# The masked softmax of a graph attention layer: subtraction and exponential by pairs of heads or by single heads

## The chip, the cores and the metric

The kernel runs on one NeuronCore of one Trainium2 chip. The metric is the device time of one execution in microseconds (us). One execution was taken by the hardware profiler; times in the trace count from the start of its span.

The engines are called as the profile calls them: PE is TensorE (PEld its weight loads), DVE is VectorE, ACT is ScalarE, POOL is GpSimd, SP is the engine whose queue issues the DMAs. A `q` behind the name is the engine's sequencer, which waits and issues.

## The reference

64 graphs of 256 nodes with 512 features each pass four layers. Every layer normalises the rows, applies relu, and adds its result to the rows. The change lies in the second layer, an attention with 8 heads over the graph's edges:

```python
feats = jnp.einsum('bnf,hfu->bhnu', X, W)
e_self = jnp.einsum('bhnu,hu->bhn', feats, a_self)
e_neigh = jnp.einsum('bhnu,hu->bhn', feats, a_neigh)
dense = e_self[..., :, None] + e_neigh[..., None, :]
dense = jax.nn.leaky_relu(dense, negative_slope=0.2)
dense = dense + NEG_BIG * (1.0 - A[:, None, :, :])
att = jax.nn.softmax(dense, axis=-1)
out = jnp.einsum('bhij,bhju->bhiu', att, feats) + b[None, :, None, :]
...
return jax.nn.relu(out)
```

All data are float32. The softmax runs over j, the neighbours of node i.

## The kernel before

The program is fully unrolled over the 64 graphs. The work of a graph is cut into 209 named steps; each step is a Python function that emits one or a few instructions. A table (`TIMES`) gives every step a due time; the steps of graph b are due `b * PERIOD` later, so several graphs are under way at once, one in each layer. `Plan.run` emits all steps in the order of their due times, with tables of their own for the first nine and the last eight graphs, and ties each engine's instructions to that order. [...]

Tiles come from pools (`g.take`) and go back (`g.done`) when their last user has run. Waits between engines follow from which slices of a tile an instruction writes and reads.

In the attention the eight heads are handled as four pairs, p = 0 to 3, with heads h = 2p + s for s = 0, 1. For a pair the tile `e{p}` holds 2 heads x 2 halves of the 256 neighbours j (128 partitions each) x 256 nodes i: 128 partitions x 1024 columns. The steps on it, with their lines:

- `ea{p}` (L1445, ACT): four instructions, leaky relu of the sum of the two scores, one for each head and half.
- `eg{p}` (L1453, POOL): two instructions of 512 columns, one for each head, add the mask (`negt`).
- `eb{p}` (L1459, DVE): one instruction of 1024 columns subtracts the maxima, which lie in the tile `m{p // 2}` (one row of 256 for each head, read twice, for both halves).
- `ex{p}` (L1465, ACT): one instruction of 1024 columns, the exponential.
- `po{p}` (L1477, PE): four matmul calls, which the profile shows as eight instructions, multiply with the features; in the order half 0 head 0, half 0 head 1, half 1 head 0, half 1 head 1.
- `eh{p}` (L1488, POOL): one instruction adds the two halves of both heads, for the softmax's sums; `su{q}` (L1502, PE) goes on with them.

The maxima are found without forming the scores: `max0` to `max3` (L1407, DVE) take them over masked neighbour scores, and they travel by DRAM to all partitions (`mr`, `mb0`, `mb1`).

The order of the pairs in the steady table is not the order of p. Around the change each engine's own order is, for the graphs between the first nine and the last eight (steps of other layers belong to other graphs):

- DVE: `tv0` (L1658, products of the third layer, read from PSUM), `eb2`, `sq1` (L1012, transposes of the normalised rows), `eb0`, `eb1`, `eb3`, `xe1` (L1560), `xe2` (L1565), `xe3` (L1570), `sqo`/`sqy` transposes (L1270), later `sq0` (L1012) and, some 15 us further on, `fe4` (L1368).
- ACT: `hn1` (L1103, the normalised rows of the second layer), `ex2`, `ta0` (L1665, tanh of the third layer), `ex0`, `ex1`, `ex3`, then `sm0`, `sx0` and `rs0` (L1072, L1082, L1088), the normalisation of a later graph's rows, and `hn0`.
- POOL: `pw1`, `sh1` (L1092, L1097, L1098: scale and shift of the normalisation, on two columns), `eg1` (L1453), `eh0`, `eh1` (L1488), `gsa` (L1172, L1173), `pw0`, `sh0`.
- PE: a product of the third layer, `po2`, `py0` (L1648), `po0`, `po1`, `po3`, `su0`, then products of the other layers (L1188).

Of the kernel before, what the change touches and what calls it, by code (L numbers as in the profile page):

```python
# [10 lines left out]
AF = mybir.ActivationFunctionType  # L11
OP = mybir.AluOpType
# [4 lines left out]
P = 128  # L17
D = 512
KC = D // P
N = 256  # L20
NC = N // P
# [705 lines left out]
class Graph:  # L727
# [5 lines left out]
    def step(self, name):  # L733
        def add(run):
            self.steps[name] = run
            return run
        return add
# [21 lines left out]
def tile_four_gnn_layers(ctx: ExitStack, tc: tile.TileContext, x, adj, nodemask,  # L759
# [6 lines left out]
    nc = tc.nc  # L766
# [253 lines left out]
    def graph(b):  # L1020

        g = Graph(plan)
# [415 lines left out]
        def attention(p):  # L1438
            @step(f"ea{p}")
            def _():  # L1440
                e = g.take("pair", 2, name=f"e{p}")
                for s in range(2):
                    h = 2 * p + s
                    for j in range(NC):
                        nc.scalar.activation(e[:, s, j, :], g[f"s{h // HA}"][:, h % HA, :], AF.Prelu,  # L1445
                                             bias=st["ec"][:, j, H + h:H + h + 1], alpha=0.2)
                g.done(f"s{p // 2}")

            @step(f"eg{p}")
            def _():  # L1450
                e = g[f"e{p}"]
                for s in range(2):
                    nc.gpsimd.tensor_tensor(e[:, s], e[:, s], g["negt"], OP.add)  # L1453
                g.done("negt")

            @step(f"eb{p}")
            def _():
                e = g[f"e{p}"]
                nc.vector.tensor_tensor(e, e, g[f"m{p // 2}"][:, p % 2 * 2:p % 2 * 2 + 2, None, :].to_broadcast([P, 2, NC, N]),  # L1459
                                        OP.subtract)  # L1460
                g.done(f"m{p // 2}")

            @step(f"ex{p}")
            def _():
                nc.scalar.activation(g[f"e{p}"], g[f"e{p}"], AF.Exp)  # L1465


            @step(f"po{p}")
            def _():
                e, q = g[f"e{p}"], p // 2  # L1470
                if p % 2 == 0:
                    g.take("bank", name=f"o{q}")
                po = g[f"o{q}"].rearrange("p (r n) -> p r n", r=2)
                for j in range(NC):
                    for s in range(2):
                        h = 2 * p + s
                        nc.tensor.matmul(po[s * U:(s + 1) * U, p % 2, :],  # L1477
                                         g[f"feats{j}"][:, E + h * U:E + (h + 1) * U],
                                         e[:, s, j, :], start=(j == 0), stop=(j == NC - 1))
                g.done(f"e{p}")  # L1480
                for j in range(NC):
                    g.done(f"feats{j}")


            @step(f"eh{p}")
            def _():
                e = g[f"e{p}"]
                nc.gpsimd.tensor_tensor(g.take("half", name=f"h{p}"), e[:, :, 0, :], e[:, :, 1, :], OP.add)  # L1488
                g.done(f"e{p}")
# [273 lines left out]
```

## Time and profile before

| | |
|---|---|
| time before | 3662.05 us, median of 3 runs (3653.04 to 3664.11) |
| profiled execution | 3662.73 us, its span 3660.9 us |
| granted TensorE clock, mean over the span | 0.981 |
| instructions in the trace | 61887 |
| idle time ahead of L1477 (PE) until L1465 has ended | 99.4 us, 58 times |
| idle time ahead of L1465 (ACT) until L1459 has ended | 28.7 us, 25 times |
| idle time ahead of L1488 (POOL) until L1465 has ended | 128.8 us |
| DMA | 785.31 MB, mean 215 GB/s |

How to read the profile's lines. A line of a group names the source line, the engine, the operation, the tiles out<-in, the shape and the count; then follow the busy time in us and the mean duration of one instruction in ns; then the idle time of the engine just before these instructions and what ended most of it. A line of the waits says who waited for whom: us in total, how many times, and the longest wait. A line of the timeline has the start in us, the length in us of all the instructions merged in the line, the engine, line and operation, the count, and in square brackets the idle time before it with what ended it. A busy engine in these lists can also be one whose instruction has started and is held up.

### The profile page before, as it was taken

To read this page: it belongs to the slowest core of one execution; us is meant where nothing else is said; L and a number is where in the kernel's file an instruction comes from. 1 tells how busy PE (TensorE), PEld (TensorE's weight loads), DVE (VectorE), ACT (ScalarE), POOL (GpSimd) and SP (SyncE) were. 2 spreads that over 40 slices of the span, in tenths; PEclk is the share of its full clock that TensorE was granted. 3 is DMA by queue.
4 is the path that set the end of the run, shared out by engine and by line. 5 is a ranking of instruction groups with operands and counts; after the bars stand their busy time and mean duration, and the time that the engine had idled before them with its cause. 6 is when DMAs were issued, how large, how long until landed. Compare 5 with 4: busy or idle time off the path is not lost.

```text
span 3660.9 us, 61887 instructions
## 1 busy us (share of the span) xinstructions
PE 3404.0 (93%) x16834; PEld 2175.1 (59%) x16834; DVE 3278.9 (90%) x8248; ACT 2780.4 (76%) x6533; POOL 2313.9 (63%) x2708
## 2 busy tenths in 40 slices
PE   5688999999999999999999999999999999999988
PEld 3455655666666666666666666666666666555554
DVE  6789998999999999999999999999989999999985
ACT  2667787787787788788778778778778778777765
POOL 3565666666666666676676666666666666566663
PEclk8789999999999999999999999999999999999999
DMA  6667667777777777777777777777777777777663
GB/s 187 181 183 216 203 215 219 222 222 222 224 219 221 228 226 218 231 222 226 219 224 221 230 223 222 228 222 221 224 219 225 223 223 229 208 212 216 197 191 119
DMA packets 995146, 785.31 MB, mean 215 GB/s; under 512 B 791984, under 2 KB 862192, under 8 KB 994800
## 3 DMA queue, kind: packets, MB, share of 16 engines
q1 hardware_dynamic: 994800, 781.35, 70.9%
q8 instruction: 137, 2.24, 0.2%
q14 instruction: 209, 1.71, 0.1%
HBM read 511.12 MB, written 270.01 MB: 213 GB/s over the span
## 4 chain that ended last, share of the span: by engine, by line
DVE 20%; PE 19%; POOL 18%; issue 13%; DMA 11%; ACT 7%; SPq 5%; POOLq 0%; ACTq 0%; DVEq 0%
PE bank L1188 13%; DMA big<-sq_d 6%; SPq L1017 4%; DVE junk L1407 4%; DVE big L1459 3%; POOL big L1453 3%; DVE big L1202 3%; PE bank L1477 3%; DVE big L1012 2%; POOL rstd L1092 2%; POOL big L1173 2%; POOL big L1172 2%; DMA sq_d<-big 2%; POOL big L1179 2%; POOL mid L1488 2%
## 5 line engine op out<-in xcount | busy, mean ns | idle before, releaser
L1188 PE MATMUL bank<-t_s,big 128*128 128x264 f32 (+3 forms) x3072 | 978.9, 452 | 8.0 <-DVE big L1658 5.7
L1188 PE MATMUL bank<-w_s,big 128*128 128x264 f32 (+2 forms) x3072 | 847.1, 409 | 44.5 <-DMA big<-sq_d 35.7
L1188 PEld LDWEIGHTS bank<-t_s,big 128*128 128x128 f32 x3072 | 582.0, 193 | 308.2 <-issue 176.7
L1188 PEld LDWEIGHTS bank<-w_s,big 128*128 128x128 f32 x3072 | 582.1, 195 | 273.9 <-issue 131.0
L1453 POOL TENSOR_TENSOR big<-big,mid 128x512 f32<-128x512 f32 x512 | 649.0, 1294 | 42.9 <-ACT big L1445 33.0
L1012 DVE STREAM_TRANSPOSE big<-big 128x512 f32<-128x512 f32 x640 | 483.5, 782 | 147.1 <-ACT big L1103 147.0
L1092 POOL TENSOR_TENSOR rstd<-rstd,power 128x2 f32<-128x2 f32 x256 | 183.6, 717 | 641.0 <-ACT rstd L1088 584.3
L1103 ACT ACTIVATE big<-big,shift,rstd 128x512 f32<-128x512 f32 x512 | 387.8, 805 | 171.7 <-POOL shift L1098 171.2
L1172 POOL TENSOR_TENSOR big<-big 128x256 f32<-128x256 f32 x256 | 226.6, 885 | 437.3 <-DMA big<-sq_d 288.1
L1407 DVE CUSTOM_DVE_ANT_0 junk<-big,bank 128x256 f32<-128x256 f32 x1024 | 428.9, 419 | 33.9 <-DMA big<-er_d 2.8
L1488 POOL TENSOR_TENSOR mid<-big 128x512 f32<-128x512 f32 x256 | 376.1, 1490 | 128.9 <-ACT big L1465 128.8
L1082 ACT ACTIVATE big<-big,sum 128x512 f32<-128x512 f32 x512 | 363.8, 711 | 111.4 <-DVE sum L1333 82.6
L1445 ACT ACTIVATE big<-big,ec 128x256 f32<-128x256 f32 x1024 | 428.8, 496 | 3.8 <-DMA big<-er_d 1.2
L1202 DVE TENSOR_TENSOR big<-bank,big 128x320 f32<-128x320 f32 (+1 forms) x704 | 399.2, 571 | 23.2 <-PE bank L1188 17.9
L1477 PE MATMUL bank<-big,big 128*64 128x256 f32 x2048 | 261.6, 390 | 103.8 <-ACT big L1465 99.4
L1459 DVE TENSOR_TENSOR big<-big,big 128x1024 f32<-128x1024 f32 x256 | 326.0, 1312 | 6.5 <-DMA big<-m_d 6.3
L1634 PE MATMUL bank<-big,big 64*128 64x256 f32 x2048 | 286.0, 400 | 45.9 <-DVE mx L1407 27.4
L1658 DVE TENSOR_TENSOR big<-bank,mid 128x512 f32<-128x512 f32 x512 | 320.9, 679 | 0.8 <-PE bank L1634 0.7
L1665 ACT ACTIVATE big<-big 128x512 f32<-128x512 f32 x512 | 291.3, 619 | 13.3 <-DVE big L1658 10.9
L1634 PEld LDWEIGHTS bank<-big,big 64*128 64x128 f32 x2048 | 221.6, 198 | 127.4 <-ACT big L1622 58.7
L1465 ACT ACTIVATE big<-big 128x1024 f32<-128x1024 f32 x256 | 267.9, 1052 | 38.0 <-DVE big L1459 28.7
L1537 ACT ACTIVATE big<-big,rs 128x64 f32<-128x64 f32 x1024 | 257.4, 334 | 27.1 <-DVE rs L1526 13.7
(132 smaller groups left out, 5839.8 us busy)
## 6 DMA issues: line engine op xcount, KB each, us to landing
sq_d<-big SPq DMA_DIRECT2D x448, 512.0 KB
big<-sq_d SPq DMA_DIRECT2D x1792, 128.0 KB
big<-er_d SPq DMA_DIRECT2D x256, 512.0 KB
big<-m_d SPq DMA_DIRECT2D x128, 512.0 KB
big<-in_x_dram SPq DMA_DIRECT2D x64, 512.0 KB
out_dram<-big SPq DMA_DIRECT2D x64, 512.0 KB
mid<-in_adj_dram SPq DMA_DIRECT2D x64, 256.0 KB
mid<-in_adj_dram SPq DMA_DIRECT2D x256, 64.0 KB
```

The costliest lines, as they stand in the source:

```text
L1012: nc.vector.transpose(sq.rearrange("p (r k i c) -> p c k r i", r=4, k=KC, c=NC)[:, c], t[:, c])
L1082: nc.scalar.activation(g["hn"][:, c, :], g["xt"][:, c, :], AF.Square, scale=-float(D), bias=st["sum"][:, c:c + 1], accum_out=st["ssq"][:, ...
L1103: nc.scalar.activation(g["hn"][:, c, :], g["xt"][:, c, :], AF.Relu, bias=st["shift"][:, c:c + 1], scale=st["rstd"][:, c:c + 1])
L1188: nc.tensor.matmul(p, a()[:, k], w[:, k], start=(k == 0), stop=(k == 1))
L1202: nc.vector.tensor_tensor(out(), g[i][:, :w], old(), OP.add)
L1407: nc.vector.tensor_tensor_reduce(junk, g[f"n{h // HA}"][:, h % HA, :], g["far"][:, c * N:(c + 1) * N], 1.0, -BIG, OP.add, OP.max, g["mx"][ ...
L1445: nc.scalar.activation(e[:, s, j, :], g[f"s{h // HA}"][:, h % HA, :], AF.Prelu, bias=st["ec"][:, j, H + h:H + h + 1], alpha=0.2)
L1453: nc.gpsimd.tensor_tensor(e[:, s], e[:, s], g["negt"], OP.add)
L1459: nc.vector.tensor_tensor(e, e, g[f"m{p // 2}"][:, p % 2 * 2:p % 2 * 2 + 2, None, :].to_broadcast([P, 2, NC, N]), OP.subtract)
L1477: nc.tensor.matmul(po[s * U:(s + 1) * U, p % 2, :], g[f"feats{j}"][:, E + h * U:E + (h + 1) * U], e[:, s, j, :], start=(j == 0), stop=(j = ...
L1488: nc.gpsimd.tensor_tensor(g.take("half", name=f"h{p}"), e[:, :, 0, :], e[:, :, 1, :], OP.add)
L1634: nc.tensor.matmul(ps[s][:, m, :], chunk(g["xpt"][half, p], m), g["xc"][half, p, :], start=True, stop=True)
```

## The change

`eb{p}` and `ex{p}` loop over the two heads of the pair. Each subtraction and each exponential now covers one head, 512 columns, and there are two of each where there was one. The order of the steps, the tiles, the values and all else stay.

```diff
             @step(f"eb{p}")
             def _():
                 e = g[f"e{p}"]
-                nc.vector.tensor_tensor(e, e, g[f"m{p // 2}"][:, p % 2 * 2:p % 2 * 2 + 2, None, :].to_broadcast([P, 2, NC, N]),
-                                        OP.subtract)
+                for s in range(2):
+                    m = g[f"m{p // 2}"][:, p % 2 * 2 + s, None, :]
+                    nc.vector.tensor_tensor(e[:, s], e[:, s], m.to_broadcast([P, NC, N]), OP.subtract)
                 g.done(f"m{p // 2}")
 
             @step(f"ex{p}")
             def _():
-                nc.scalar.activation(g[f"e{p}"], g[f"e{p}"], AF.Exp)
+                for s in range(2):
+                    nc.scalar.activation(g[f"e{p}"][:, s], g[f"e{p}"][:, s], AF.Exp)
```

## The prediction

> **What bounds the kernel now.** I read the page first: which engines are full, and what stands before and behind the two changed lines.
>
> ```profile
> PE 3404.0 (93%) x16834; PEld 2175.1 (59%) x16834; DVE 3278.9 (90%) x8248; ACT 2780.4 (76%) x6533; POOL 2313.9 (63%) x2708
> ...
> L1459 DVE TENSOR_TENSOR big<-big,big 128x1024 f32<-128x1024 f32 x256 | 326.0, 1312 | 6.5 <-DMA big<-m_d 6.3
> ...
> L1658 DVE TENSOR_TENSOR big<-bank,mid 128x512 f32<-128x512 f32 x512 | 320.9, 679 | 0.8 <-PE bank L1634 0.7
> L1665 ACT ACTIVATE big<-big 128x512 f32<-128x512 f32 x512 | 291.3, 619 | 13.3 <-DVE big L1658 10.9
> ...
> L1465 ACT ACTIVATE big<-big 128x1024 f32<-128x1024 f32 x256 | 267.9, 1052 | 38.0 <-DVE big L1459 28.7
> ```
>
> TensorE and VectorE are both nearly full, so neither alone is the answer. The instruction list of L1459 shows that the first of a graph's four subtractions starts at 706.00 us in graph 11 and at 3043.80 in graph 54, 54.37 us apart on average, and that the four keep their distances within about 0.02 us in these 44 graphs. One period can therefore stand for them; I take the one from 1467.38 to 1521.55. Its waits:
>
> ```profile
> ACT big L1103 <- POOL shift L1098: 2.7, 2, 1.4
> DVE big L1012 <- ACT big L1103: 2.6, 2, 1.4
> ...
> PE bank L1477 <- ACT big L1465: 1.4, 1, 1.4
> ...
> DVE bank L1368 <- PE bank L1188: 0.4, 1, 0.4
> ```
>
> TensorE's longest wait is for an exponential; VectorE waits for the normalised rows, which wait for GpSimd; and at L1368 VectorE waits 0.4 us for TensorE. After that VectorE runs with no wait of note to the next period. So whatever makes TensorE later at the attention makes L1368 later and the period longer, one for one. Now the timeline of the attention, engine by engine (start, length of the whole line, count):
>
> ```profile
> 1467.47 1.18 POOL L1097 TENSOR_TENSOR shift<-sum,rstd 128x2 f32<-128x2 f32 x1
> 1468.73 0.20 POOL L1098 TENSOR_TENSOR shift<-shift,share_of 128x2 f32<-128x2 f32 x1
> ...
> 1473.64 3.49 POOL L1488 TENSOR_TENSOR mid<-big 128x512 f32<-128x512 f32 x2 [2.25 <-ACT big L1465]
> ```
> ```profile
> 1467.38 1.22 DVE L1459 TENSOR_TENSOR big<-big,big 128x1024 f32<-128x1024 f32 x1
> 1469.81 1.42 DVE L1012 STREAM_TRANSPOSE big<-big 128x512 f32<-128x512 f32 x2 [1.21 <-ACT big L1103]
> 1471.15 3.59 DVE L1459 TENSOR_TENSOR big<-big,big 128x1024 f32<-128x1024 f32 x3
> ```
> ```profile
> 1468.96 1.52 ACT L1103 ACTIVATE big<-big,shift,rstd 128x512 f32<-128x512 f32 x2 [1.31 <-POOL shift L1098]
> 1470.39 1.04 ACT L1465 ACTIVATE big<-big 128x1024 f32<-128x1024 f32 x1
> 1471.34 1.14 ACT L1665 ACTIVATE big<-big 128x512 f32<-128x512 f32 x2
> 1472.51 3.33 ACT L1465 ACTIVATE big<-big 128x1024 f32<-128x1024 f32 x3
> ```
> ```profile
> 1471.48 1.08 PE L1477 MATMUL bank<-big,big 128*64 128x256 f32 x8 [1.44 <-ACT big L1465]
> ...
> 1474.12 2.93 PE L1477 MATMUL bank<-big,big 128*64 128x256 f32 x24
> ```
>
> The point to see: L1097 is an instruction on two columns, mostly 0.20 us, but here it lasts 1.18 us and ends just after eb2, which started 0.09 us before it. The first L1488 (eh0) starts 0.11 us after eb3 (1473.53) and ends 1.15 us after it. GpSimd and a subtraction of two SBUF operands exclude each other. Who gets in when two subtractions stand back to back is shown early in the run:
>
> ```profile
> 196.29 5.64 DVE L1459 TENSOR_TENSOR big<-big,big 128x1024 f32<-128x1024 f32 x3
> ```
> ```profile
> 196.67 4.17 POOL L1453 TENSOR_TENSOR big<-big,mid 128x512 f32<-128x512 f32 x2
> ```
>
> Three subtractions take 5.64 us and not 3.59: single ones take 1.18, 2.31 and 2.30, and the two L1453 run in the two gaps. A waiting GpSimd instruction goes in at the boundary, and the next subtraction pays 1.10 us (2.31 less the median of 1.21). In all eleven places where a GpSimd instruction of 256 or 512 columns waited at such a boundary, it went first. The change puts a new boundary into every subtraction.
>
> **The change part by part.**
>
> Instructions. 256 VectorE instructions become 512 and 256 ScalarE instructions become 512; nothing else is added, removed or reordered, no DMA, and no queue is passed. A subtraction of 512 columns I take from L1658: 0.68 us, the next starting 0.60 later (four in 2.47 us). A pair lasts 1.28 against 1.21: 0.07 more. No row has the subtraction itself at 512; the ends are half of its 1.21 (a pair then costs nothing) and L1063, 512 columns with two SBUF operands, whose 805 ns contain the times it is held up (a pair then costs 0.4). L1658 is the nearest in operation and size, so I take it. An exponential of 512 is like L1665: 0.61, the next after 0.52 (two in 1.13 to 1.14). A pair lasts 1.13 against 1.04, but its first half is there 0.43 earlier. Were each 0.07 on the path, 256 would cost 18 us; on ScalarE 256 times 0.09 is 23 us, but ScalarE is 76% busy.
>
> The first head, eb2 to po2. L1097 no longer waits for all of eb2. The first half ends at 1468.06, L1097 gets in and ends 0.05 later, at 1468.11. L1098 comes 0.08 later and finds the second half (1467.98 to 1468.66) at work; it ends 0.05 after that, 1468.71, against 1468.93 now. So hn1 and all that follows start 0.21 earlier (1468.75 instead of 1468.96). Po2's first products can start after one half; the last wait for the second half, 1470.70 to 1471.32. TensorE leaves po2 0.34 us earlier (six of eight products left at 1471.37, 0.11 each, against eight at 1471.48).
>
> eb0, eb1, eb3. From 1470.94 (1471.15 less 0.21), with the 0.10 that L1453 holds up eb0 now, the halves start at 1470.94, 1471.64, 1472.24, 1472.84, 1473.44 and 1474.04; undisturbed the last ends at 1474.72, where it ends now (1474.74). ScalarE: ex2 at 1470.18 and 1470.70, L1665 at 1471.22 and 1471.74, ex0 at 1472.26 and 1472.78 to 1473.39; eh0 comes 0.08 after that, at 1473.47, some 0.02 after the first half of eb3. It waits for that half (to 1474.12) and then runs ahead of the second half. Today nothing of VectorE that reads two SBUF operands stands behind eb3, so the same wait costs VectorE nothing. Then, the second half of eb3 ends at 1474.04 + 0.68 + 1.10 = 1475.82, 1.08 later than now. Queued behind it on VectorE are xe1 to xe5 and the transposes (L1560, L1565, L1270); VectorE has 1.4 us of idle time before L1012 at 1481.01, which covers 1.08. Ex3's second half runs 1475.85 to 1476.48 instead of ending at 1475.84: ScalarE is 0.64 later, and with it sm0, sx0, rs0 and hn0, for which VectorE waits at 1481.01. Po3 now starts its eight products at 1475.88; then its last six start at 1476.53, and TensorE is free at 1477.19 against 1476.76: 0.43 later. That has eaten the 0.34 that po2 gave.
>
> The meeting point. At L1368 VectorE comes 0.64 later but had waited 0.41, so it is 0.23 late; TensorE is 0.43 late. The later one counts: 0.43 us per period. In 44 graphs that is 19 us. In the other 20 the order differs; the like waits there (eh0 held 0.55 to 0.7 us by eb3 in graphs 4 to 7) bound them by 0 and by about 1 us each, and I take the same 0.43: 9 us. Sum 28 us. The profiled execution took 3662.7 us (span 3660.9), 0.7 from the median of 3662.05, so 3662 + 28 = 3690.
>
> A rule against this reading: the Trainium skill (Perfetto Trace Analysis, Optimizing Scalar/DVE Operations) says that where ScalarE and VectorE aren't saturated but cause bubbles on other engines, breaking up instructions may let work finish sooner. By it the 1.44 us bubble before po2 should shrink and the sum be a gain, some 15 us by the 0.34 above; with VectorE at 90% its condition hardly holds, and the rows of 196.29 decide for me.
>
> **Rivals.**
>
> 1. eh0 gets in one boundary earlier. My margin is 0.02 us. For: a subtraction at 3274.91 yielded to a GpSimd instruction that started 0.05 before it. Against: at 252.89 one won against an L1098 that had started 0.02 to 0.03 before. Then both halves of eb3 pay 1.10 (eh0 ahead of the first, eh1 ahead of the second): eb3 ends 2.2 later, ex3 1.76, TensorE 1.53 late at L1368. 44 times 1.53 is 67 us, with 0.5 for each of the others 77: 3739.
>
> 2. Faster: GpSimd does not get in between the halves. The next VectorE instruction starts 0.08 before its predecessor ends, which could close the gap for shorter ones. Then eb3 ends as now, ex3 ends 0.43 earlier, po3 follows po1 0.34 earlier, and each period is 0.34 shorter: 15 us in 44 graphs, 22 in all 64, 3640 to 3647. It decides as soon as eb3 pays less than 0.43 us. Against: eleven of eleven.
>
> 3. The loss is mostly covered. If TensorE recovers its 0.43 before L1368, VectorE's own 0.23 stays: 10 to 15 us, or, with some graphs untouched, under the 11 us (0.3%) that a measurement of this kernel can tell from no change. Against: TensorE has no wait between po3 and 1489.5.
>
> 4. The exponential still waits for both halves, so that the overlap does not arise. Against: L1665 starts at 1515.33, before the second L1658 of its pair ends at 1515.84, with the same slices by head. Ex3 would end 0.5 us later still (0.52 and 0.61 after 1475.85), 22 us in 44 graphs: about 3715.
>
> **How the numbers follow.** Forecast 0.50 (with small shifts about it, 3675 to 3710), rival 1 0.18, rival 4 0.05, rival 3 0.14, rival 2 0.13. Predicted 3690. The range runs from 3655, which leaves out most of rival 2, to 3745, above rival 1 with its unknown 20 graphs. Below 3651 lies rival 2: 0.13; within 0.3%: most of rival 3: 0.12; the rest is slower: 0.75.
>
> **What would show it.** Right: L1459 x512 with a mean of 0.8 to 0.9 us and not 0.68, a second half of eb3 near 1.8 us, L1097 after eb2 near 0.65 us, hn1 starting 1.37 us after eb2 (now 1.58), a period near 54.8 us, L1488 with a shorter mean. Wrong: all halves at 0.68 (rival 2), or both halves of eb3 at 1.8 (rival 1), or a changed period while eb3 is undisturbed.

## The result and the profile after

The changed kernel takes 3690.86 us (median, 3688.71 to 3695.31); the kernel before, on the same chip in the same comparison, 3658.78. The ratio is 1.0084, 95% interval 1.0071 to 1.0097: 0.8% slower. The prediction was 3690 us. The profiled execution took 3695.31 us with a span of 3693.5, at a mean granted clock of 0.984 (before: 3662.73, 3660.9, 0.981). From 700 to 3050 us it is 1.00 in both, so the clock is no part of the loss. All lines behind the change shift by two.

The page after, engines and groups:

```profile
PE 3433.0 (93%) x16834; PEld 2137.8 (58%) x16834; DVE 3354.7 (91%) x8504; ACT 2795.9 (76%) x6789; POOL 2300.8 (62%) x2708
...
L1461 DVE TENSOR_TENSOR big<-big,big 128x512 f32<-128x512 f32 x512 | 414.2, 866 | 7.2 <-DMA big<-m_d 7.1
...
L1467 ACT ACTIVATE big<-big 128x512 f32<-128x512 f32 x512 | 289.1, 618 | 78.6 <-DVE big L1461 78.3
...
L1660 DVE TENSOR_TENSOR big<-bank,mid 128x512 f32<-128x512 f32 x512 | 320.7, 677 | 0.9 <-PE bank L1636 0.5
```

Two VectorE instructions of the same size stand here. L1660, with one operand in PSUM, keeps its 0.68 us. L1461, with both in SBUF, has a mean of 866 ns. An undisturbed L1461 takes 0.68 too (below), so the mean holds time in which it was held up. The exponential waits 78.3 us for it instead of 28.7.

The graph whose first subtraction starts at 1479.75, on VectorE, GpSimd, ScalarE and TensorE in turn (start, length of the whole line, count):

```profile
1479.75 1.28 DVE L1461 TENSOR_TENSOR big<-big,big 128x512 f32<-128x512 f32 x2
1481.97 1.42 DVE L1012 STREAM_TRANSPOSE big<-big 128x512 f32<-128x512 f32 x2 [0.94 <-ACT big L1103]
1483.31 4.88 DVE L1461 TENSOR_TENSOR big<-big,big 128x512 f32<-128x512 f32 x6
```
```profile
1479.84 0.65 POOL L1097 TENSOR_TENSOR shift<-sum,rstd 128x2 f32<-128x2 f32 x1
1480.56 0.52 POOL L1098 TENSOR_TENSOR shift<-shift,share_of 128x2 f32<-128x2 f32 x1
...
1485.84 3.49 POOL L1490 TENSOR_TENSOR mid<-big 128x512 f32<-128x512 f32 x2 [2.29 <-ACT big L1467]
```
```profile
1484.63 2.69 ACT L1467 ACTIVATE big<-big 128x512 f32<-128x512 f32 x5
1488.22 0.63 ACT L1467 ACTIVATE big<-big 128x512 f32<-128x512 f32 x1 [0.90 <-DVE big L1461]
```
```profile
1488.91 1.08 PE L1479 MATMUL bank<-big,big 128*64 128x256 f32 x6 [0.46 <-ACT big L1467]
1489.91 0.64 PE L1504 MATMUL bank<-mid,ones 128*32 128x256 f32 x8
```

The gain is there: L1097 lasts 0.65 instead of 1.18, as it goes in between the two halves of eb2. So is the loss: six halves of eb0, eb1 and eb3 need 4.88 us where three whole subtractions needed 3.59. Five exponentials run without a gap, then ScalarE waits 0.90 for the last half of eb3, and TensorE waits 0.46 for that exponential.

Over graphs 11 to 54 the instruction list of L1461 gives a period of 54.837 us; before it was 54.367. In the medians of these graphs the second half of eb3 takes 1765 ns and each other half 678 to 682, except the first of eb0, which L1453 holds up (789). The span is 32.6 us longer: 43 periods of 0.47 make 20.2, graphs 0 to 11 add 5.1, graphs 54 to 63 8.6, and the ends take off 1.2.

### The profile page after: what moved, and what is told of

Read it like the earlier page. It is cut to its first block, busy times and chain, and to the rows that moved or that the text cites. A ratio compares the mean times of both kernels' runs of the same rounds, so it can differ in the third digit from the quotient of the medians.

```text
span 3693.5 us, 62315 instructions
## 1 busy us (share of the span) xinstructions
PE 3433.0 (93%) x16834; PEld 2137.8 (58%) x16834; DVE 3354.7 (91%) x8504; ACT 2795.9 (76%) x6789; POOL 2300.8 (62%) x2708
## 4 chain that ended last, share of the span: by engine, by line
DVE 24%; PE 20%; POOL 19%; issue 14%; DMA 11%; ACT 7%; SPq 5%; POOLq 0%; DVEq 0%; ACTq 0%
PE bank L1188 15%; DVE big L1461 7%; DMA big<-sq_d 7%; SPq L1017 4%; DVE junk L1407 4%; POOL big L1453 3%; DVE big L1012 3%; POOL rstd L1092 3%; DVE big L1202 2%; POOL big L1173 2%; POOL big L1172 2%; POOL big L1179 2%; POOL big L1180 2%; ACT big L1082 2%; POOL mid L1490 2%
## 5 line engine op out<-in xcount | busy, mean ns | idle before, releaser
L1188 PE MATMUL bank<-t_s,big 128*128 128x264 f32 (+3 forms) x3072 | 978.2, 452 | 6.9 <-DVE big L1660 5.5
L1188 PE MATMUL bank<-w_s,big 128*128 128x264 f32 (+2 forms) x3072 | 849.0, 409 | 43.4 <-DMA big<-sq_d 36.1
L1188 PEld LDWEIGHTS bank<-t_s,big 128*128 128x128 f32 x3072 | 580.4, 193 | 308.4 <-issue 191.8
L1188 PEld LDWEIGHTS bank<-w_s,big 128*128 128x128 f32 x3072 | 577.8, 195 | 279.8 <-issue 154.8
L1453 POOL TENSOR_TENSOR big<-big,mid 128x512 f32<-128x512 f32 x512 | 648.4, 1292 | 46.3 <-ACT big L1445 34.4
L1490 POOL TENSOR_TENSOR mid<-big 128x512 f32<-128x512 f32 x256 | 375.0, 1485 | 138.9 <-ACT big L1467 137.0
L1461 DVE TENSOR_TENSOR big<-big,big 128x512 f32<-128x512 f32 x512 | 414.2, 866 | 7.2 <-DMA big<-m_d 7.1
L1479 PE MATMUL bank<-big,big 128*64 128x256 f32 x2048 | 316.2, 392 | 102.3 <-ACT big L1467 99.6
L1467 ACT ACTIVATE big<-big 128x512 f32<-128x512 f32 x512 | 289.1, 618 | 78.6 <-DVE big L1461 78.3
L1660 DVE TENSOR_TENSOR big<-bank,mid 128x512 f32<-128x512 f32 x512 | 320.7, 677 | 0.9 <-PE bank L1636 0.5
L1667 ACT ACTIVATE big<-big 128x512 f32<-128x512 f32 x512 | 291.3, 618 | 12.7 <-DVE big L1660 10.6
L1479 PEld LDWEIGHTS bank<-big,big 128*64 128x64 f32 x2048 | 166.1, 138 | 232.6 <-ACT big L1467 172.0
```

Source lines behind the costliest of these rows:

```text
L1188: nc.tensor.matmul(p, a()[:, k], w[:, k], start=(k == 0), stop=(k == 1))
L1461: nc.vector.tensor_tensor(e[:, s], e[:, s], m.to_broadcast([P, NC, N]), OP.subtract)
L1479: nc.tensor.matmul(po[s * U:(s + 1) * U, p % 2, :], g[f"feats{j}"][:, E + h * U:E + (h + 1) * U], e[:, s, j, :], start=(j == 0), stop=(j = ...
```

## The experiments

The theory: a GpSimd instruction that waits for a subtraction goes in at the next boundary, and the subtraction behind it pays. The split put a boundary into eb3, just where eh0 waits. The table has the medians of the regular graphs, in us after the start of eb2. "Last product" is the start of the last matmul of po3, "TensorE goes on" the first L1188 behind the sums. The ratios go to the kernel before, which had a median of 3658.78 to 3663.43 in the four comparisons.

| kernel | total | ratio (95%) | period | last subtraction of eb3 | ex3 ends | last product | eh1 ends | TensorE goes on | L1368 starts |
|---|---|---|---|---|---|---|---|---|---|
| before | 3662.05 | | 54.37 | 1.21 (whole) | 8.45 | 9.29 | 9.73 | 10.34 | 22.15 |
| after | 3690.86 | 1.0084 (1.0071 to 1.0097) | 54.84 | 1.77 | 9.11 | 9.86 | 9.58 | 10.74 | 22.62 |
| eb_only | 3719.34 | 1.0157 (1.0143 to 1.0171) | 55.22 | 1.76 | 9.53 | 10.29 | 9.57 | 11.17 | 23.05 |
| ex_only | 3657.53 | 0.9989 (0.9980 to 0.9999) | 54.41 | 1.21 (whole) | 8.54 | 9.38 | 9.74 | 10.35 | 22.16 |
| eb3_whole | 3664.35 | 1.0006 (0.9998 to 1.0015) | 54.09 | 1.21 (whole) | 8.48 | 9.23 | 9.67 | 10.28 | 22.09 |
| ex2_whole | 3742.45 | 1.0220 (1.0204 to 1.0235) | 55.91 | 1.76, and 1.76 the half before | 10.19 | 10.94 | 8.97 | 11.81 | 23.70 |
| before_thin_eh | 3646.44 | 0.9959 (0.9947 to 0.9971) | 54.26 | 1.21 (whole) | 8.44 | 9.29 | 8.16 | 10.17 | 21.97 |
| after_thin_eh | 3638.49 | 0.9941 (0.9928 to 0.9953) | 54.13 | 0.68 | 8.09 | 9.18 | 7.56 | 10.05 | 21.86 |
| after_pilot | 3665.84 | 1.0009 (1.0000 to 1.0018) | 54.20 | 0.68 | 8.09 | 9.17 | 9.74 | 10.35 | 22.15 |
| eb2_halves | 3648.91 | 0.9965 (0.9953 to 0.9978) | 54.14 | 1.21 (whole) | 8.24 | 9.08 | 9.53 | 10.14 | 21.94 |
| eb2_quarters | 3660.42 | 0.9999 (0.9990 to 1.0008) | 54.10 | 1.21 (whole) | 8.19 | 8.94 | 9.47 | 10.08 | 21.89 |

**Each half of the change alone.** `eb_only` splits the subtraction and leaves the exponential whole:

```diff
                 for s in range(2):
                     m = g[f"m{p // 2}"][:, p % 2 * 2 + s, None, :]
                     nc.vector.tensor_tensor(e[:, s], e[:, s], m.to_broadcast([P, NC, N]), OP.subtract)
...
-                for s in range(2):
-                    nc.scalar.activation(g[f"e{p}"][:, s], g[f"e{p}"][:, s], AF.Exp)
+                nc.scalar.activation(g[f"e{p}"], g[f"e{p}"], AF.Exp)
```

> The subtraction is split by head, the exponential stays whole. Theory (a waiting GpSimd instruction enters at the new boundary): eh0 still comes just after the first half of eb3 has started, the second half of eb3 lasts near 1.8 us, and ex3, now whole, can start only after it and ends 1.1 us later than in the kernel before. The period grows by 1.0 to 1.1 us: 44 us in the 44 regular graphs and some 10 in the others, 3705 to 3725 us, slower than the whole change. Rival (the price is the added instructions themselves, 0.07 to 0.09 us each): half of the instructions, half of the loss, 3672 to 3677 us.

`ex_only` is the reverse: the whole subtraction of before, and two exponentials.

> The exponential is split by head, the subtraction stays whole. Theory: no new boundary on VectorE, eb3 stays at 1.21 us, eh0 waits behind it as before, TensorE gains at po2 what ScalarE loses; 3652 to 3664 us, within 0.2% of before. Rival (added instructions): 256 times 0.09 us, 3670 to 3682 us.

The subtraction carries all of the loss. Alone it costs 1.6%; the split exponential alone, with its 256 more ScalarE instructions, moves the time by 0.1%. Together they lose less than the subtraction alone, for the split exponential lets ex3's first half run while the second half of eb3 is held up: ex3 ends at 9.11 instead of 9.53.

**Where in the subtraction.** `eb3_whole` is the changed kernel with only eb3 in one piece:

```diff
-                for s in range(2):
-                    m = g[f"m{p // 2}"][:, p % 2 * 2 + s, None, :]
-                    nc.vector.tensor_tensor(e[:, s], e[:, s], m.to_broadcast([P, NC, N]), OP.subtract)
+                if p == 3:
+                    nc.vector.tensor_tensor(e, e, ...)      # one instruction, as before
+                else:
+                    ...                                     # two halves, as after
```

> The whole change, except that the subtraction of the pair p = 3 stays one instruction of 1024 columns. Theory: eh0 again has to wait until all of eb3 has run, the loss is gone, and what is left are the small gains of the first head: 3648 to 3662 us. Rival (added instructions): seven eighths of the loss stay on VectorE and all on ScalarE, about 3685 us.

`ex2_whole` is the changed kernel with one instruction fewer per graph: ex2 is a single exponential again. It is 0.09 us shorter than two, and so eh0 comes 0.09 us earlier.

```diff
-                for s in range(2):
-                    nc.scalar.activation(g[f"e{p}"][:, s], g[f"e{p}"][:, s], AF.Exp)
+                if p == 2:
+                    nc.scalar.activation(g[f"e{p}"], g[f"e{p}"], AF.Exp)
+                else:
+                    for s in range(2):
+                        nc.scalar.activation(g[f"e{p}"][:, s], g[f"e{p}"][:, s], AF.Exp)
```

> The whole change, except that the exponential of the pair p = 2 stays one instruction. ScalarE does one instruction less per graph, and eh0 comes 0.09 us earlier, which is enough to be ahead of the first half of eb3. Theory: both halves of eb3 then pay 1.1 us (first eh0, then eh1 gets in), the period grows by about 1.1 us over that of the whole change: 3730 to 3750 us. Rival (added instructions): 64 times 0.09 us less than the change, about 3685 us.

In the regular graphs one boundary decides. With eb3 whole their loss is gone: the period falls to 54.09, and L1368 starts at 22.09 against 22.15 before. The total, 3664, lies just above what I expected, and it is even only because two things cancel: graphs 0 to 11 and 54 to 63 still take 3.1 and 7.6 us more than before, where the whole change had added 5.1 and 8.6. There the order of the steps differs, and GpSimd instructions of 256 or 512 columns go in between subtractions at other places: 11 times in the trace of before, 33 times in that of `after`, 28 times in that of `eb3_whole`. What these are worth was not tested. With ex2 whole the loss more than doubles. The timeline of `ex2_whole`, VectorE and GpSimd:

```profile
1502.83 5.96 DVE L1461 TENSOR_TENSOR big<-big,big 128x512 f32<-128x512 f32 x6
```
```profile
1505.26 2.97 POOL L1493 TENSOR_TENSOR mid<-big 128x512 f32<-128x512 f32 x2 [2.20 <-ACT big L1470]
```

Six halves now take 5.96 us instead of 4.88. In the medians eh0 starts 6.00 us after eb2, while the last half of eb1 is at work, and goes in ahead of the first half of eb3; eh1 goes in ahead of the second. In the changed kernel eh0 started at 6.088, when the first half of eb3 had been at work for 0.012. Those 0.09 us are worth 1.07 us per period. This is the first rival of the prediction come true in another kernel: it was priced at 1.53 per period and 3739 us, and `ex2_whole` is 1.54 per period slower than before and takes 3742.

The traces of all twelve kernels show how far ahead GpSimd must be where two subtractions stand back to back. An instruction of 256 or 512 columns that had started at least 0.07 us before the second subtraction went first in 487 of 488 places (the exception is at 106.22 in `ex2_whole`). Where the lead was 0.04 us or less, it never did.

**Without the opponent.** In this pair eh0 to eh3 read only two columns and a memset fills the rest, in the kernel before and in the changed one:

```diff
-                nc.gpsimd.tensor_tensor(g.take("half", name=f"h{p}"), e[:, :, 0, :], e[:, :, 1, :], OP.add)
+                h = g.take("half", name=f"h{p}")
+                nc.gpsimd.memset(h, 1.0)
+                nc.gpsimd.tensor_tensor(h[:, :, :2], e[:, :, 0, :2], e[:, :, 1, :2], OP.add)
```

> The kernel before with a thin eh: a memset of the tile and a sum over two columns of each head, so the sums of the softmax are left out; the wait for the exponentials stays. It is the reference of the next run. GpSimd's reading part is short, so eh0 hardly holds the port. Both theories: a little faster than before, since su0 need not wait for eh1: 3640 to 3658 us.

> The changed kernel with the same thin eh (the sums of the softmax are left out). Theory: with nothing long waiting on GpSimd the second half of eb3 lasts 0.7 to 0.8 us, ex3 ends 0.4 us and po3 0.3 us earlier than in the run before this one, and the change turns into a gain of 10 to 22 us against it. Rival (added instructions): the loss stays as it was, some 32 us slower than the run before this one.

With nothing large waiting at the boundary, the second half of eb3 takes 0.68, and the loss is gone. The same split now gains a little: 3638.49 against 3646.44, 0.2%, though the two intervals overlap. The gain is smaller than expected. The first product of po0 starts 0.36 us earlier, but the last of po3 only 0.11. In `before_thin_eh` the products of po2 start in pairs 7 ns apart, those of po0 and po1 in turn 177 and 39 ns apart, and the 24 of po0, po1 and po3 take 2.55 us from the first start to the last. In `after_thin_eh`, where po2 has waited for each half (3.46 and 3.73), the first two and the last two of these 24 stand alone, 0.21 to 0.22 us from their neighbours (the last is 0.09 behind in `before_thin_eh`), the others in pairs, and the 24 take 2.80. `ex_only` shows the same pattern. Why the pattern costs this was not tested.

**The opponent made short.** If a waiting instruction costs the next subtraction only its own length, a short one put ahead of eh0 should take its place at the boundary:

```diff
+                if p == 0:
+                    h = g.take("half", name=f"h{p}")
+                    nc.gpsimd.tensor_tensor(h[:, :, :2], e[:, :, 0, :2], e[:, :, 1, :2], OP.add)
+                    nc.gpsimd.tensor_tensor(h, e[:, :, 0, :], e[:, :, 1, :], OP.add)
```

> The changed kernel, with one more GpSimd instruction: ahead of eh0 the same sum is taken once over its first two columns alone (128x2x2), so that a short GpSimd instruction stands at the boundary inside eb3 and the whole eh0 behind it. Nothing is left out. Theory (whoever waits goes in at the boundary, and the subtraction behind it pays for that instruction's length): the short one comes 0.01 us after the first half of eb3 began, goes in at the boundary and costs the second half under 0.2 us instead of 1.09; the whole eh0 then finds the second half at work, as L1098 does after L1097 in eb2, waits for its end and costs VectorE nothing. eb3's second half 0.7 to 0.9 us, ex3 ends 8.1 to 8.3 us after eb2 (after: 9.11, before: 8.45), period 54.1 to 54.35 us (after: 54.84), total 3640 to 3662: an added instruction takes back the loss. Rival (the loss comes from the number of instructions, or from eh0's traffic wherever it stands): 3690 to 3705. Second rival (the whole eh0 goes in right behind the short one, ahead of the second half): eb3's second half 1.8 to 2.0, total 3690 to 3700.

```profile
1467.45 3.80 DVE L1461 TENSOR_TENSOR big<-big,big 128x512 f32<-128x512 f32 x6
```
```profile
1469.98 0.73 POOL L1492 TENSOR_TENSOR mid<-big 128x4 f32<-128x4 f32 x1 [2.29 <-ACT big L1467]
1470.79 1.60 POOL L1493 TENSOR_TENSOR mid<-big 128x512 f32<-128x512 f32 x1
```

The six halves take 3.80 us instead of 4.88, and ex3 ends at 8.09, as it does without eh0's traffic. An added instruction takes back some 25 us. But 3665.84 is not the gain that `after_thin_eh` showed, and lies just above what I expected. The table shows what holds it: TensorE goes on at 10.35, as before the change, although its last product is 0.12 earlier. The matmuls of the sums (su0) read h1, and eh1 now ends at 9.74. The timeline of TensorE, first before, then after, then `after_pilot`:

```profile
1476.99 0.82 PE L1502 MATMUL bank<-mid,ones 128*32 128x256 f32 x8
```
```profile
1489.91 0.64 PE L1504 MATMUL bank<-mid,ones 128*32 128x256 f32 x8
```
```profile
1473.38 0.93 PE L1509 MATMUL bank<-mid,ones 128*32 128x256 f32 x8
```

The eight products take 0.64 us when both sums are ready, 0.82 and 0.93 when the second must be waited for. In every kernel of the table "TensorE goes on" is, within 0.01 us, the later of two times: the last product plus 0.88, and eh1's end plus 0.61. Before and in `after_pilot` eh1 is the later; in `after`, `eb_only` and `ex2_whole` the product is. So GpSimd and eb3 exclude each other, and both orders cost: GpSimd first makes ex3 late, eb3 first makes the sums late. The mean period of the traced execution is still 0.16 us shorter than before, with L1368 at 22.15 in both; single periods before lie between 53.6 and 56.1 us, so I read nothing into that.

**Only the useful boundary.** `eb2_halves` is the kernel before with one subtraction split, eb2, so that L1097 can go in:

```diff
-                nc.vector.tensor_tensor(e, e, ...)
+                if p == 2:
+                    for s in range(2):
+                        m = g[f"m{p // 2}"][:, p % 2 * 2 + s, None, :]
+                        nc.vector.tensor_tensor(e[:, s], e[:, s], m.to_broadcast([P, NC, N]), OP.subtract)
+                else:
+                    nc.vector.tensor_tensor(e, e, ...)
```

> The kernel before with only the subtraction of the pair p = 2 in two halves. Theory: L1097 gets in between the halves and hn1 starts 0.21 us earlier after eb2, with all that follows; eb0, eb1, eb3 and eh0 keep their order. 9 us in the regular graphs, 13 at most: 3645 to 3652 us. Rival (added instructions): 64 times 0.07 us, 3660 to 3664 us.

`eb2_quarters` cuts eb2 into four pieces of 256 columns, so that L1098 need not wait for half an eb2 either.

> The kernel before with only the subtraction of the pair p = 2 in four quarters of 256 columns. Theory: L1097 gets in after the first quarter and L1098 after the second, hn1 starts 0.75 us earlier after eb2 than before, and if nothing else takes over the period shrinks by as much: 33 us in the regular graphs, 3615 to 3640 us. Rival (added instructions): 192 times 0.07 us on a nearly full VectorE, 3665 to 3675 us.

The halves do what they should: eh1's end, TensorE's going on and L1368 all come 0.21 us earlier, and the kernel is 0.35% faster than before. The quarters missed, and by the same rule. VectorE and GpSimd of `eb2_quarters`:

```profile
1462.18 2.49 DVE L1462 TENSOR_TENSOR big<-big,big 128x256 f32<-128x256 f32 x4
```
```profile
1462.27 0.38 POOL L1097 TENSOR_TENSOR shift<-sum,rstd 128x2 f32<-128x2 f32 x1
1462.73 0.26 POOL L1098 TENSOR_TENSOR shift<-shift,share_of 128x2 f32<-128x2 f32 x1
1462.94 2.87 POOL L1453 TENSOR_TENSOR big<-big,mid 128x512 f32<-128x512 f32 x2
```

L1098 is done by 1462.99, but L1453 (512 columns) stands behind it and goes in ahead of the fourth quarter, which takes 1.50 us instead of 0.42. The transposes sq1 start 2.42 us after eb2, as before the change. I had followed the two short instructions and not the third one in the queue. The period still falls by 0.27, and the first and last graphs, 2.7 and 7.1 us longer, take it back.

**No boundary needed.** `eb2_early` is the kernel before with no split; eb2 stands ahead of the two products L1658 on VectorE and is done before L1097 comes:

```diff
-"eb2": 43.450
+"eb2": 41.900
```

> The kernel before, with no subtraction split; only eb2 is put earlier in the written order of VectorE (its due time 41.90 instead of 43.45), so that it stands ahead of the two products of L1658 and is done when L1097 comes. Theory (L1097 and L1098 are late only because eb2 is at work when they come): both last about 0.20 us, hn1 starts some 0.9 us earlier against the work before it, the period falls by up to 0.9 us if nothing else gets late, total 3616 to 3650. It is half a gain at best if the products of L1658, 1.2 us later, hold up ScalarE's L1665 and what follows: then 3650 to 3665. Rival (the wait of L1097 is worth nothing since TensorE sets the pace): 3655 to 3668 with hn1 earlier and L1368 not.

```profile
1460.53 0.20 POOL L1097 TENSOR_TENSOR shift<-sum,rstd 128x2 f32<-128x2 f32 x1
1460.80 0.20 POOL L1098 TENSOR_TENSOR shift<-shift,share_of 128x2 f32<-128x2 f32 x1
```
```profile
1458.66 1.23 DVE L1459 TENSOR_TENSOR big<-big,big 128x1024 f32<-128x1024 f32 x1 [1.20 <-DMA big<-m_d]
1459.80 2.48 DVE L1658 TENSOR_TENSOR big<-bank,mid 128x512 f32<-128x512 f32 x4
```

The two short instructions are no longer held up (median 0.20 us each). The total is 3633.91 us, ratio 0.9919 (0.9906 to 0.9933): the fastest kernel here. The period is 53.87, 0.50 less than before. Hn1 starts 0.28 us earlier against the L1368 before it, not the 0.9 that I had hoped for at most. It has another wait now. Before, hn1 starts 0.04 us after L1098 has ended, in every regular graph; here 0.61 us after (median), and in every regular graph it follows L1665 on ScalarE without a gap. So the expectation's own doubt came true: the products L1658, put behind eb2, hold up L1665, and hn1 stands behind that. The idle time ahead of L1665 until L1658 has ended is 49.1 us in the whole trace, 10.9 before. ScalarE of `eb2_early`:

```profile
1460.52 1.23 ACT L1665 ACTIVATE big<-big 128x512 f32<-128x512 f32 x2 [1.52 <-DVE big L1658]
1461.66 1.50 ACT L1103 ACTIVATE big<-big,shift,rstd 128x512 f32<-128x512 f32 x2
```

Ahead of eb2 in this chain stands the transfer of the maxima. Idle time of VectorE ahead of L1459, by what ended it, before and then in `eb2_early` (us, times):

```profile
  DMA big<-m_d: 6.3, 2
```
```profile
  DMA big<-m_d: 32.2, 40
```

Eb2, put earlier, now waits for its maxima in most graphs, with a median of 0.49 us. Whether an earlier transfer would gain was not tested.

## Why the prediction was right, point by point

- **The entry at the boundary.** Right for the regular graphs, and shown from both sides: their loss goes when the boundary is closed (`eb3_whole`) and when a short instruction stands at it (`after_pilot`), and doubles when eh0 comes one boundary earlier (`ex2_whole`). The margin was 0.012 us, where I had worked out 0.02.
- **Sizes.** The second half of eb3 1.77 (predicted near 1.8), the mean of L1461 0.866 (0.8 to 0.9), L1097 0.65, hn1 1.371 after eb2 (1.37), ex3 0.66 late (0.64), the period 54.84 (near 54.8). One sign did not come: the mean of L1488 was to be shorter and is 1485 ns instead of 1490, for eh0 is 0.44 us shorter but eh1, which now waits for the second half of eb3, 0.45 longer.
- **From ex3 to TensorE.** Right in the sum, wrong in two terms that cancel in part. I let po3's six products after the wait take 0.22 less than the eight before. From ex3's end to the start of the last product it is 0.75 against 0.84, only 0.09 less, so the last product is 0.57 late and not 0.43. But TensorE had already been waiting 0.18 for eh1 before the change. I had not looked for that wait (rival 3 even argued from there being none after po3), and the new lateness hides it: 0.57 less 0.18 is the 0.39 by which TensorE goes on later (10.34 to 10.74). By L1368 it has grown to 0.47; where the other 0.08 comes from was not traced. That 0.43 lies so near 0.47 is in part luck. VectorE's own 0.23 of rival 3 was too much: L1368 starts 0.47 later with a wait 0.03 longer, so VectorE came only 0.45 late, 0.03 more than its old wait.
- **The other 20 graphs.** The step assumed 9 us; the span gives 12.5. The size is near by luck: the sum took the same wait at eb3 for them, but with eb3 whole 10.7 of the 13.6 us stay (`eb3_whole`). What costs there is open.
- **The total.** 3690 against 3690.86 is closer than the working deserves. The sum added 28 us to 3662; measured, the change costs 32 us on a kernel before that took 3658.78 in this comparison.
- **Rival 2 was too generous.** Even with no entry at the boundary the 0.34 per period would not have come: `after_thin_eh` gains 0.14 per period against its own base (0.11 at L1368), and with eh1 in place, in `after_pilot`, TensorE gains nothing at the sums.
- **Rival 4** is excluded by `eb_only`: with one exponential per pair ex3 ends 0.42 later than with two, so the halves do overlap.
- **The rule against the reading.** The Trainium skill (Perfetto Trace Analysis, Optimizing Scalar/DVE Operations) lets breaking up instructions bring work forward where engines are not saturated but cause bubbles elsewhere. Here the same kind of split gives +1.6% (all subtractions), −0.1% (the exponentials) and −0.35% (eb2 alone). For the subtractions, what decided was which GpSimd instruction stood at the new boundary.
- **A page that fits.** L1461, with two SBUF operands, is held up by GpSimd and L1660, with one, keeps 677 ns: in the trace of `after`, 230 of its 512 ran wholly beside a GpSimd instruction of 256 or 512 columns, with a median of 674 ns, and 245 beside none, with 679. The Trainium skill (SBUF — State Buffer, Who interferes with whom) states just this, and that the order of issue decides who blocks. The runs here add by how much the first must be ahead (0.07 us against 0.04, above).

## What to carry to other kernels

Before a VectorE instruction with both operands in SBUF is cut in two, list what is queued on GpSimd when it starts. Here the first waiting instruction went in at the cut, and the second half paid 1.09 us for one that takes 1.28 alone. Cut where a short instruction that others wait for is held up and nothing long stands behind it; leave whole what a long one would break into, or move the instruction out of the way, which here gained more than any cut. Then ask who waits for the one that lost: here either order had a consumer on TensorE.

## What was not expected

- With eb3 whole, the regular graphs lose nothing, but the other 20 keep 10.7 of the 13.6 us that the whole change had cost them.
- TensorE waited for eh1 already before the change. These 0.18 us cover a part of the loss in the changed kernel, and in `after_pilot` they take what the sooner end of ex3 gives.
- In `eb2_quarters` the boundaries meant for two short instructions let in the long one behind them: the fourth quarter takes 1.50 us instead of 0.42.
